# Two slots of a scan made in one tile, the product with B issued for both at once, and the projection weights loaded pass by pass

## The chip, the cores and the metric

The kernel runs on one core of a Trainium2 chip. The metric is device time in microseconds (us), from the first to the last instruction of one launch. A core has five engines that run their own instruction streams in order: PE (TensorE, matrix products), DVE (VectorE), ACT (ScalarE), POOL (GpSimd) and SP (SyncE, which here issues every DMA). They meet through semaphores. SBUF is the on-chip memory of 128 partitions, PSUM holds the results of PE in banks.

## What is computed

Two layers on an image of 8 samples, 512 channels and 48 x 48 = 2304 positions. Layer 0 adds to x a linear attention with a causal sum over the positions (8 heads of 64 channels). Layer 1 adds a chain of four state-space blocks, one for each 128 channels. Each layer first normalizes x by groups of 16 channels.

```python
# layer 0, with x0 = _gn(x)
q  = einsum('nchw,oc->nohw', x0, Wq) + bq ;  kv = einsum('nchw,oc->nohw', x0, Wkv) + bkv
Q, K = elu(q) + 1, elu(k) + 1                    # per head, positions in order
num = q_l . sum_{m<=l} k_m v_m^T ;  den = 1 / (Q . cumsum(K) + 1e-10)
x = x + num * den
# layer 1, block i of 4, on x_i = spx[i] + prev
xz = u @ Wi.T ;  xp, z = split(xz)               # 256 inner channels d
xs = silu(causal_conv4(xp) + bc)
dt, Bm, Cm = split(xs @ Wx.T)                    # 8, 16 and 16 rows
delta = softplus(dt @ Wdt.T + bdt)
h_l = exp(delta_l * A) * h_(l-1) + (delta_l * xs_l) * Bm_l      # 256 x 16 states
y = (h . Cm + xs * D) * silu(z) ;  x_m = y @ Wo.T
fused = max(x_i, x_m) ; feature = sigmoid(mean(x_i)) * x_i + sigmoid(mean(fused)) * fused
```

The state of layer 1 is a recurrence over 2304 positions for each of 8 samples x 4 blocks x 256 channels x 16 states. It is most of the work around the change.

## The kernel before

**Jobs and slots.** A sample's 2304 positions are cut into `NC` = 6 chunks of `LC` = 384. A *job* is one chunk of one block of one sample: 8 x 4 x 6 = 192 jobs. Two streams (even and odd samples) take turns; a stream's jobs follow one another, since each needs the last states of the one before. A job has `SLOTS` = 8 slots, 1536 in all. A slot holds four scans of 128 partitions x 384 positions: `NG` = 2 pairs of states, times 2 groups of channels. Slots 0 to 3 belong to one half of the channels, 4 to 7 to the other, and slot s uses state group s % 4.

**One slot.** The tile `u` holds the input of the four scans, then their result, then the result times C:

- `last_product` (L849): ACT copies the states kept from the chunk before into column 0 (L855), POOL makes the product of B and `dxr` for the last `TAIL` = 128 positions (L856);
- `product` (L864): DVE makes it for the first 256 positions (L867);
- `decay` (L873): ACT makes exp(delta A) into a PSUM bank (L877), `DEPTH` = 3 of them ahead;
- `scan` (L885): DVE runs the recurrence in place (L888), four times a slot;
- `weigh` (L898): POOL saves the last state (L902) and multiplies the tile by C in place (L904);
- `gather` (L908): PE adds it into `yp` (L911).

**Order.** The order on each engine is written out by hand in `slot` (L1130). In slot k it first issues `product` for slot k+1, then the four scans of slot k. After the second scan it issues the `gather` of slot k-2, then `last_product` for slot k+2 (L1161), and after the scans `weigh`. So POOL gets, slot after slot: product for k+2, other work, `weigh` of k. At slot 7 both of the next job's first two `product`s are issued (L1164). `u` has five buffers. `prime` (L1120) makes the first two slots where nothing was issued ahead.

**Work beside the slots.** Other work is written as generators that yield the place where they go on; a place is a half slot. `beside` (L1051) is called twice a slot and lets those go on that are due and find PSUM banks. `hurry` forces them. `Job.prepare` (L681) makes conv, gate, xs and delta of a job and loads its inputs. With `first` = twice the job's first slot, its DMAs go out at fixed half slots: steps of delta `dr` (`steps`), delta times xs `dxr` (`scaled`) and the rows of B and C, each spread over 64 partitions from a scratch tensor in DRAM (`rows`, L794). There are four tiles of B and four of C for a job, one for each state group, of two rows each; tile q serves slots q and q + 4. A tile takes two DMAs of 192 KB. Before that, delta goes to DRAM (`spread`, L771), POOL multiplies it by xs in place (L805) and it goes to DRAM again. Stores wait in a list and are issued by `flush` (L167) two half slots later. All DMAs are on the queue of SP.

**Attention.** `chunk` (L273) does one of 192 chunks (sample b, 128 output channels o, chunk c) of layer 0: three projections on PE (L293) with weights from `wq_sb`, and the rest of the attention in some thirty half slots. `statistics` (L216) makes the group sums of a sample; for the first sample it loads x whole into tiles of the tag `u`. The projection weights are all loaded at the start, 12 DMAs of 256 KB by `load_projections` (L106), into one tile of 4 x 1536 columns. `fetch` (L258) loads the normalized x of the next chunk.

The tiles are handed out by a pool: a tag has a number of buffers, and a new tile waits for the last user of the buffer that it takes. The waits between engines come from which parts of a tile an instruction reads and writes.

Of the kernel before, what the change touches and what calls it, by code (L numbers as in the profile page):

```python
# [9 lines left out]
F32 = mybir.dt.float32  # L10
# [7 lines left out]
P = 128  # L18
# [32 lines left out]
def attention_then_mamba_kernel(  # L51
# [50 lines left out]
    wq_sb = cpool.tile([P, 4, 1536], F32, name="wq_sb")  # L102
# [3 lines left out]
    def load_projections(o):  # L106

        src = wqkv.rearrange("(t p) c -> p t c", p=P)
        for j in range(3):
            cols = slice(j * 512 + o * P, j * 512 + (o + 1) * P)  # L110
            nc.sync.dma_start(out=wq_sb[:, :, cols], in_=src[:, :, cols])
# [104 lines left out]
    def statistics(b):  # L216
# [3 lines left out]
        if b == 0:  # L220

            xs = []

            def load(c):
                t = mpool.tile([P, 4, 1 + LC], F32, tag="u", name=f"xs_{c}", bufs=5)[:, :, 0:LC]
                nc.sync.dma_start(out=t, in_=xv[:, :, c * LC : (c + 1) * LC])
                xs.append(t)

            for c in range(5):
                load(c)  # L230
            load_projections(0)
            for c in range(NC):
                for ct in range(4):
                    nc.vector.bn_stats(stats[:, ct, c, :], xs[c][:, ct, :])
                if c == 0:
                    load(5)
                    fetch(0)
            for o in range(1, 4):
                load_projections(o)
# [33 lines left out]
    def chunk(m):  # L273
# [16 lines left out]
        def project(j):  # L290
            ps = bank()[:, 0:LC]
            for kt in range(4):
                nc.tensor.matmul(  # L293
                    ps,
                    wq_sb[:, kt, j * 512 + o * P : j * 512 + (o + 1) * P],
# [44 lines left out]
        fetch(m + 1)  # L340
        if o:
# [156 lines left out]
    class Stream:  # L498
# [62 lines left out]
        def pass_on(self):  # L561
# [52 lines left out]
            if last and self.z:  # L614

                got = [
                    mpool.tile([P, 4, 1 + LC], F32, tag="u", name=f"end_{i}", bufs=5)
                    for i in range(NC // 2)
                ]
                for c in range(NC):  # L620
# [53 lines left out]
    class Job:  # L674
# [6 lines left out]
        def prepare(self):  # L681
# [98 lines left out]
            src = scr.rearrange("(q i m f) l -> q m i (f l)", q=4, m=2, i=2)  # L780
# [13 lines left out]
            def rows(m, q):  # L794
                t = mpool.tile([P, NG, LC], F32, tag="BC"[m], name=f"{'BC'[m]}_{n}_{q}", bufs=4)
# [20 lines left out]
            rows(0, 1)  # L816
            self.prepared = True
            yield first - 3, 0
            rows(0, 2)
            yield first - 2, 0  # L820
            rows(1, 0)
            yield first - 1, 0
            rows(0, 3)
            yield first, 0
            rows(1, 1)
# [3 lines left out]
            rows(1, 2)  # L829
            yield first + 3, 0  # L830
            steps(1)
            yield first + 4, 0
            rows(1, 3)

        prepared = closed = False

# [12 lines left out]
        def last_product(self, s):  # L849

            shape, cols = [P, NG, 2, TAIL], slice(LC - TAIL, LC)
            u = mpool.tile([P, NG, 2, 1 + LC], F32, tag="u", name=f"u_{self.n}_{s}", bufs=5)
            if self.c:
                h, q = s // 4, s % 4 * NG
                nc.scalar.copy(u[:, :, :, 0], self.state[:, h, q : q + NG, :])  # L855
# [403 lines left out]
```

## Time and profile before

Three runs took 8785.19, 8786.02 and 8791.31 us, with a median of 8786.02. The profiled execution has a span of 8790.1 us.

| | us |
|---|---|
| median of three runs | 8786.02 |
| span of the profiled execution | 8790.1 |
| first scan | some 229 after the start |
| scans on DVE, L888, 6144 of 939 ns | 5457.0 |
| product with C on POOL, L904, 1536 of 3179 ns | 4882.7 |
| decays on ACT, L877, 6144 of 578 ns | 3413.6 |
| gather on PE, L911, 12288 of 519 ns | 2440.7 |
| product with B on POOL, L856, 1536 of 1277 ns | 1960.9 |
| product with B on DVE, L867, 1536 of 1195 ns | 1836.0 |
| projections on PE, L293, 4608 of 508 ns | 1680.1 |

How to read a group's line: line of the kernel, engine, operation, output and inputs by the program's names with their shapes, count, then busy time in all and the mean of one in ns, then the engine's idle time ahead of these instructions, and what ended it. A line of the waits reads: engine and line, what it waited for, us in total, how often, the longest. The chain is followed back from the last instruction to what released each step; its shares are shares of the span.

The 16 DMA engines are busy 69.0% of the span with the data queue and move 1642.98 MB, of which the rows of B and C are 3072 transfers of 192 KB.

### The profile page before, as it was taken

What the parts mean: (1) busy time and instruction counts of PE and PEld (TensorE: products, weight loads), DVE (VectorE), ACT (ScalarE), POOL (GpSimd) and SP (SyncE); (2) the same over time, 40 slices, a digit from 0 to 9 for tenths busy, and PEclk for the clock granted to TensorE, in tenths of its full rate; (3) what the DMA queues carried; (4) which work ended last, traced back from release to release, by engine and by line L of the source; (5) the groups of instructions that cost most, each with busy time, mean ns of one, the idle gap of its engine ahead of it and who ended that gap; (6) DMA issues with size and microseconds to landing.
All of it is one profiled execution on the core that took longest, in us unless ns stands there. A gap on an engine that the chain in (4) does not pass through costs nothing.

```text
span 8790.1 us, 122627 instructions
## 1 busy us (share of the span) xinstructions
PE 7766.8 (88%) x36482; PEld 3705.4 (42%) x36482; DVE 8067.0 (92%) x11078; ACT 6744.5 (77%) x13220; POOL 8044.8 (92%) x5623
## 2 busy tenths in 40 slices
PE   7899999998899899998889999999888999999865
PEld 4444444444444444444444444444444444444422
DVE  2899999999899999998889999999889999999998
ACT  2777887777788878777778878877777888877875
POOL 1789999999999999999999999999999999999998
PEclk9999999999999999999999999999999999999977
DMA  5667777766676777776667677777667666766655
GB/s 184 166 174 189 193 197 195 190 188 186 190 191 188 191 195 198 196 190 189 179 190 192 188 191 198 198 195 188 188 183 191 189 187 187 189 187 185 183 156 144
DMA packets 1002907, 1642.98 MB, mean 187 GB/s; under 512 B 138592, under 2 KB 797312, under 8 KB 1002240
## 3 DMA queue, kind: packets, MB, share of 16 engines
q1 hardware_dynamic: 1002240, 1635.13, 69.0%
q8 instruction: 291, 4.77, 0.2%
q14 instruction: 376, 3.08, 0.1%
HBM read 1309.06 MB, written 325.58 MB: 186 GB/s over the span
## 4 chain that ended last, share of the span: by engine, by line
DVE 28%; POOL 20%; ACT 14%; DMA 13%; PE 13%; issue 7%; SPq 4%; POOLq 0%; DVEq 0%; ACTq 0%
DVE u L888 19%; POOL u L904 11%; ACT bank L877 5%; DVE u L867 5%; POOL u L856 4%; PE bank L693 4%; PE bank L293 3%; PE yp L911 3%; DMA C<-scr 3%; SPq L797 2%; DMA dscr<-delta 2%; ACT L877 2%; DMA B<-scr 1%; ACT L764 1%; POOL delta L805 1%
## 5 line engine op out<-in xcount | busy, mean ns | idle before, releaser
L888 DVE TENSOR_TENSOR_SCAN u<-bank,u 128x385 f32<-128x385 f32 (+1 forms) x6144 | 5457.0, 939 | 350.1 <-ACT bank L877 300.3
L904 POOL TENSOR_TENSOR u<-u,C 128x1536 f32<-128x1536 f32 x1536 | 4882.7, 3179 | 121.9 <-DVE gm_m L182 16.9
L877 ACT ACTIVATE bank<-dr,av 128x385 f32<-128x385 f32 (+1 forms) x6144 | 3413.6, 578 | 752.3 <-DVE u L888 611.9
L911 PE MATMUL yp<-u,cst 128*64 128x384 f32 x12288 | 2440.7, 519 | 428.2 <-POOL u L904 355.9
L856 POOL TENSOR_TENSOR u<-B,dxr 128x512 f32<-128x512 f32 x1536 | 1960.9, 1277 | 16.5 <-DMA dxr<-xscr 13.8
L867 DVE TENSOR_TENSOR u<-B,dxp 128x1024 f32<-128x1024 f32 x1536 | 1836.0, 1195 | 11.3 <-ACT dxp L840 11.1
L293 PE MATMUL bank<-xn,wq_sb 128*128 128x384 f32 x4608 | 1680.1, 508 | 82.2 <-POOL xn L317 40.1
L911 PEld LDWEIGHTS yp<-u,cst 128*64 128x64 f32 x12288 | 782.0, 140 | 1660.6 <-issue 842.6
L693 PE MATMUL bank<-xi,wk 128*128 128x384 f32 x3072 | 1117.8, 507 | 218.5 <-ACT kl L390 112.5
L293 PEld LDWEIGHTS bank<-xn,wq_sb 128*128 128x128 f32 x4608 | 849.0, 195 | 826.5 <-DVE u L888 119.6
L693 PEld LDWEIGHTS bank<-xi,wk 128*128 128x128 f32 x3072 | 560.6, 192 | 780.8 <-ACT kl L390 202.1
L805 POOL TENSOR_TENSOR delta<-delta,xs 128x384 f32<-128x384 f32 x384 | 384.4, 1001 | 278.0 <-DMA dscr<-delta 215.9
L305 ACT ACTIVATE ex<-bank,bqkv_sb 128x384 f32<-128x384 f32 x384 | 221.0, 576 | 523.8 <-PE bank L293 523.6
L877 ACT ACT_TABLE_LOAD x382 | 490.1, 1283 | 6.7
L845 ACT ACTIVATE yp<-xs,pv 128x384 f32<-128x384 f32 x384 | 223.8, 583 | 290.8 <-DVE yz L923 289.3
L902 POOL COPY state<-u 128x4 f32<-128x4 f32 x1280 | 242.4, 189 | 172.6 <-DVE u L888 170.0
L753 PE MATMUL bank<-dbc,wd 9*128 9x384 f32 x768 | 315.6, 532 | 1.2 <-ACT dbc L745 1.1
L929 PE MATMUL bank<-yz,wo 128*128 128x384 f32 x768 | 299.2, 506 | 18.5 <-DVE yz L923 14.6
L704 PE MATMUL bank<-xi,wi 128*128 128x384 f32 x768 | 285.9, 494 | 10.9 <-ACT xs L729 10.9
L740 PE MATMUL bank<-xs,wx 128*40 128x384 f32 x768 | 281.0, 489 | 2.6 <-ACT sm L457 2.6
L923 DVE TENSOR_TENSOR yz<-yp,sz 128x384 f32<-128x384 f32 x384 | 211.6, 551 | 62.5 <-PE yp L911 62.3
L423 PE MATMUL bank<-cst,rdb 128*128 128x128 f32 x576 | 113.0, 311 | 170.7 <-DVE u L888 168.5
(117 smaller groups left out, 8018.7 us busy)
## 6 DMA issues: line engine op xcount, KB each, us to landing
B<-scr SPq DMA_DIRECT2D x1536, 192.0 KB
C<-scr SPq DMA_DIRECT2D x1536, 192.0 KB
xn<-xn SPq DMA_DIRECT2D x192, 768.0 KB
dr<-dscr SPq DMA_DIRECT2D x768, 192.0 KB
dxr<-xscr SPq DMA_DIRECT2D x768, 192.0 KB
dscr<-delta SPq DMA_DIRECT2D x192, 384.0 KB
xscr<-delta SPq DMA_DIRECT2D x192, 384.0 KB
xn<-in_x SPq DMA_DIRECT2D x48, 768.0 KB
```

The costliest lines, as they stand in the source:

```text
L293: nc.tensor.matmul(ps, wq_sb[:, kt, j * 512 + o * P : j * 512 + (o + 1) * P], xn[:, kt, :], start=(kt == 0), stop=(kt == 3),)
L693: nc.tensor.matmul(xc, wk[:, k, h * P : (h + 1) * P], xi[:, c0 + k : c0 + k + LC], start=(k == 0), stop=(k == 3),)
L704: nc.tensor.matmul(zp, wi[:, 256 + h * P : 256 + (h + 1) * P], xi[:, c0 + 3 : c0 + 3 + LC], start=True, stop=True,)
L753: nc.tensor.matmul(vp, wd[32:41, h * P : (h + 1) * P], dbc[32:41, :], start=True, stop=True)
L805: nc.gpsimd.tensor_tensor(delta[:, h, :], delta[:, h, :], xs[:, h, :], ALU.mult)
L856: nc.gpsimd.tensor_tensor(u[:, :, :, 1 + LC - TAIL :], self.B[s % 4][:, :, cols].unsqueeze(2).to_broadcast(shape), self.dxr[s // 4][:, :, ...
L867: nc.vector.tensor_mul(u[:, :, :, 1 : 1 + LC - TAIL], self.B[s % 4][:, :, cols].unsqueeze(2).to_broadcast(shape), self.dxp.unsqueeze(1).to ...
L877: nc.scalar.activation(dA[:, cols], self.dr[h][:, g, cols], AF.Exp, scale=self.w[6][:, 2 * h + g, q + j : q + j + 1],)
L888: nc.vector.tensor_tensor_scan(u[:, j, g, cols], dA[:, cols], u[:, j, g, cols], 0.0, ALU.mult, ALU.add,)
L904: nc.gpsimd.tensor_tensor(h, h, self.C[s % 4].unsqueeze(2).to_broadcast([P, NG, 2, LC]), ALU.mult)
L911: nc.tensor.matmul(self.yp[g * 64 : g * 64 + 64, 0:LC], pair_sum, u[:, j, g, 1:], start=False, stop=(s % 4 == 3 and j == NG - 1), skip_gro ...
L929: nc.tensor.matmul(self.xm[:, 0:LC], self.w[2][:, h, :], self.yz[:, h, :], start=(h == 0), stop=(h == 1),)
```

## The change

`u` tiles hold two slots (8 scans) instead of one, and there are three buffers of them instead of five. `last_product` is called at even slots alone and issues one ACT copy and one POOL product for both slots; `product`, the scans, `weigh` and `gather` stay one a slot. The tiles of B and C hold four rows, two buffers each instead of four; tile q now serves slots 2q, 2q + 1, 2q + 4 and 2q + 5. Their loads go from 16 a job to 8 of twice the size, at fewer places. The projection weights come as one contiguous load for each of the 32 passes over a sample's 128 output channels, in a tile with two buffers, asked for at the last chunk but one of the pass before; the host lays them out for that. At the start the six tiles of x are all loaded before the weights.

```diff
-    wq_sb = cpool.tile([P, 4, 1536], F32, name="wq_sb")
-    def load_projections(o):
-        src = wqkv.rearrange("(t p) c -> p t c", p=P)
-        for j in range(3):
-            cols = slice(j * 512 + o * P, j * 512 + (o + 1) * P)
-            nc.sync.dma_start(out=wq_sb[:, :, cols], in_=src[:, :, cols])
+    wqs = []
+    def load_projections():
+        i = len(wqs)
+        if i < 4 * B:
+            o = parts[i * NC][1]
+            w = apool.tile([P, 4, 3 * P], F32, tag="wq", name=f"wq_{i}", bufs=2)
+            nc.sync.dma_start(out=w.rearrange("p t c -> p (t c)"), in_=wqkv[o])
+            wqs.append(w)
...
             def load(c):
-                t = mpool.tile([P, 4, 1 + LC], F32, tag="u", name=f"xs_{c}", bufs=5)[:, :, 0:LC]
+                if c % 2 == 0:
+                    both = mpool.tile([P, 8, 1 + LC], F32, tag="u", name=f"xs_{c}", bufs=3)
+                    halves.append(both)
+                t = halves[c // 2][:, c % 2 * 4 : c % 2 * 4 + 4, 0:LC]
...
-            for c in range(5):
+            for c in range(NC):
                 load(c)
-            load_projections(0)
+            load_projections()
...
-                    load(5)
                     fetch(0)
-            for o in range(1, 4):
-                load_projections(o)
...
-                    wq_sb[:, kt, j * 512 + o * P : j * 512 + (o + 1) * P],
+                    wqs[m // NC][:, kt, j * P : (j + 1) * P],
...
         fetch(m + 1)
+        if c == NC - 2:
+            load_projections()
...
-            src = scr.rearrange("(q i m f) l -> q m i (f l)", q=4, m=2, i=2)
+            src = scr.rearrange("(q i m f) l -> q m i (f l)", q=2, m=2, i=2)
...
             def rows(m, q):
-                t = mpool.tile([P, NG, LC], F32, tag="BC"[m], name=f"{'BC'[m]}_{n}_{q}", bufs=4)
+                t = mpool.tile([P, 2 * NG, LC], F32, tag="BC"[m], name=f"{'BC'[m]}_{n}_{q}", bufs=2)
...
             yield first - 5, 0
-            rows(0, 1)
             self.prepared = True
             yield first - 3, 0
-            rows(0, 2)
+            rows(0, 1)
             yield first - 2, 0
             rows(1, 0)
-            yield first - 1, 0
-            rows(0, 3)
-            yield first, 0
-            rows(1, 1)
             yield first + 1, 0
             scaled(1)
             yield first + 2, 0
-            rows(1, 2)
+            rows(1, 1)
             yield first + 3, 0
             steps(1)
-            yield first + 4, 0
-            rows(1, 3)
+        def part(self, tiles, s):
+            return tiles[s % 4 // 2][:, s % 2 * NG : s % 2 * NG + NG]
...
         def last_product(self, s):
-            shape, cols = [P, NG, 2, TAIL], slice(LC - TAIL, LC)
-            u = mpool.tile([P, NG, 2, 1 + LC], F32, tag="u", name=f"u_{self.n}_{s}", bufs=5)
+            shape, cols = [P, 2 * NG, 2, TAIL], slice(LC - TAIL, LC)
+            u = mpool.tile([P, 2 * NG, 2, 1 + LC], F32, tag="u", name=f"u_{self.n}_{s}", bufs=3)
             if self.c:
                 h, q = s // 4, s % 4 * NG
-                nc.scalar.copy(u[:, :, :, 0], self.state[:, h, q : q + NG, :])
+                nc.scalar.copy(u[:, :, :, 0], self.state[:, h, q : q + 2 * NG, :])
             nc.gpsimd.tensor_tensor(
                 u[:, :, :, 1 + LC - TAIL :],
-                self.B[s % 4][:, :, cols].unsqueeze(2).to_broadcast(shape),
+                self.B[s % 4 // 2][:, :, cols].unsqueeze(2).to_broadcast(shape),
                 self.dxr[s // 4][:, :, cols].unsqueeze(1).to_broadcast(shape),
                 ALU.mult,
             )
-            return u
+            return [u[:, 0:NG], u[:, NG : 2 * NG]]
...
-        for r in range(2):
-            us[k + r] = job.last_product(s + r)
+        us[k], us[k + 1] = job.last_product(s)
...
                 if not end and k + 2 < slots and not apart(k + 2):
                     j, r = at(k + 2)
-                    us[k + 2] = j.last_product(r)
+                    if s % 2 == 0:
+                        us[k + 2], us[k + 3] = j.last_product(r)
```

`product` and `weigh` read their part of B and C through `part`. The rows of the projection that gives B and C, and the projection weights, are laid out on the host to match. The last block's end, which borrows tiles of the tag `u`, takes parts of two of the larger tiles.

More of the change, by code (lines that the diff above doesn't have):

```diff
@@ L220, in statistics @@
         if b == 0:
-            xs = []
+            xs, halves = [], []
             def load(c):
-                t = mpool.tile([P, 4, 1 + LC], F32, tag="u", name=f"xs_{c}", bufs=5)[:, :, 0:LC]
+                if c % 2 == 0:
+                    both = mpool.tile([P, 8, 1 + LC], F32, tag="u", name=f"xs_{c}", bufs=3)
+                    halves.append(both)
+                t = halves[c // 2][:, c % 2 * 4 : c % 2 * 4 + 4, 0:LC]
                 nc.sync.dma_start(out=t, in_=xv[:, :, c * LC : (c + 1) * LC])
                 xs.append(t)
-            for c in range(5):
+            for c in range(NC):
                 load(c)
-            load_projections(0)
+            load_projections()
             for c in range(NC):
@@ L616, in pass_on @@
                 got = [
-                    mpool.tile([P, 4, 1 + LC], F32, tag="u", name=f"end_{i}", bufs=5)
-                    for i in range(NC // 2)
+                    mpool.tile([P, 2 * NG, 2, 1 + LC], F32, tag="u", name=f"end_{i}", bufs=3).rearrange(
+                        "p a b l -> p (a b) l"
+                    )
+                    for i in range(2)
                 ]
+                got = [got[0][:, 0:4], got[0][:, 4:8], got[1][:, 0:4]]
                 for c in range(NC):
@@ L868, in product @@
                 u[:, :, :, 1 : 1 + LC - TAIL],
-                self.B[s % 4][:, :, cols].unsqueeze(2).to_broadcast(shape),
+                self.part(self.B, s)[:, :, cols].unsqueeze(2).to_broadcast(shape),
                 self.dxp.unsqueeze(1).to_broadcast(shape),
@@ L904, in weigh @@
             nc.gpsimd.tensor_tensor(
-                h, h, self.C[s % 4].unsqueeze(2).to_broadcast([P, NG, 2, LC]), ALU.mult
+                h, h, self.part(self.C, s).unsqueeze(2).to_broadcast([P, NG, 2, LC]), ALU.mult
             )
@@ L1225 @@
         8 + 16 * m + 2 * (q + j) + i
-        for q in range(0, 8, NG)
+        for q in range(0, 8, 2 * NG)
         for i in range(2)
         for m in range(2)
-        for j in range(NG)
+        for j in range(2 * NG)
     ]
@@ L1233 @@
         "consts": constants(),
-        "wqkv": lay(np.concatenate([wq, wkv], axis=0).T),
+        "wqkv": lay(
+            np.concatenate([wq, wkv], axis=0)
+            .reshape(3, 4, P, 4, P)
+            .transpose(1, 4, 3, 0, 2)
+            .reshape(4, P, 4 * 3 * P)
+        ),
         "bqkv": lay(np.concatenate([bq, bkv]).reshape(12, P).T),
```

## The prediction

> **What bounds the kernel now.** I read the page's busy line first, then the groups, the chain, the windows and the waits. Two engines stand level, and a third is close:
>
> ```profile
> PE 7766.8 (88%) x36482; PEld 3705.4 (42%) x36482; DVE 8067.0 (92%) x11078; ACT 6744.5 (77%) x13220; POOL 8044.8 (92%) x5623
> DVE 28%; POOL 20%; ACT 14%; DMA 13%; PE 13%; issue 7%; SPq 4%; POOLq 0%; DVEq 0%; ACTq 0%
> DVE u L888 19%; POOL u L904 11%; ACT bank L877 5%; DVE u L867 5%; POOL u L856 4%; PE bank L693 4%; PE bank L293 3%; PE yp L911 3%; DMA C<-scr 3%; SPq L797 2%; DMA dscr<-delta 2%; ACT L877 2%; DMA B<-scr 1%; ACT L764 1%; POOL delta L805 1%
> ```
>
> DVE and POOL are both busy 92% of 8790.1 us. The chain that ended last moves among all engines, with no more than 28% on one of them. So a saving on POOL alone does not come through whole.
>
> The windows say where each is the tighter one (columns: window, length, busy of PE, weight load, DVE, ACT, POOL, clock, DMA share, GB/s):
>
> ```profile
> 1826.70:2387.20 560.50, 490.47 (x2267) 229.93 (x2267) 503.33 (x693) 421.62 (x830) 523.05 (x384) 0.95 0.69 188
> 2914.60:3440.70 526.10, 477.24 (x2286) 229.66 (x2285) 504.88 (x694) 423.35 (x831) 497.69 (x342) 0.99 0.73 194
> 8259.40:8790.00 530.60, 349.83 (x1272) 134.26 (x1271) 471.35 (x579) 357.96 (x693) 496.74 (x334) 0.81 0.57 155
> ```
>
> Each of the first two holds 96 slots. The first has more POOL work and takes 34.4 us longer with the same DVE work: POOL leads there (93.3% against 89.8%), as in the last window. Two more windows are like the first (from 3968.5 and 6117.5 us). In the other twelve or so, DVE is at about 96% and POOL at 95%. So about 384 slots are POOL's, and 1152 are DVE's first.
>
> What DVE waits for, over the whole run:
>
> ```profile
> DVE u L888 <- ACT bank L877: 300.3, 212, 4.4
> DVE q L350 <- ACT bank L306: 102.4, 57, 6.0
> DVE yz L923 <- PE yp L911: 62.3, 39, 6.6
> DVE u L888 <- POOL u L856: 49.0, 41, 2.9
> ```
>
> It waits directly for POOL only 49.0 us. But late POOL products also hold PE (the waits list gives 951 us of PE and its weight loads on L904), PE holds ACT, and ACT's decays hold the scans. Part of the first three lines is POOL's.
>
> **The change, part by part.** The prices:
>
> ```profile
> L904 POOL TENSOR_TENSOR u<-u,C 128x1536 f32<-128x1536 f32 x1536 | 4882.7, 3179 | 121.9 <-DVE gm_m L182 16.9 <-DVE u L888 0.9 <-DMA B<-scr 0.4
> L856 POOL TENSOR_TENSOR u<-B,dxr 128x512 f32<-128x512 f32 x1536 | 1960.9, 1277 | 16.5 <-DMA dxr<-xscr 13.8 <-DMA B<-scr 2.7
> L805 POOL TENSOR_TENSOR delta<-delta,xs 128x384 f32<-128x384 f32 x384 | 384.4, 1001 | 278.0 <-DMA dscr<-delta 215.9 <-ACT bank L877 33.3 <-ACT sm L457 18.8
> L539 POOL TENSOR_TENSOR wk<-wk,wi 128x256 f32<-128x256 f32 x128 | 93.2, 730 | 7.1 <-DMA wk<-in_wconv 3.6 <-DMA av<-in_alog 3.4
> L855 ACT COPY u<-state 128x4 f32<-128x4 f32 x1280 | 238.6, 186 | 5.7 <-PE yp L911 3.0
> ```
>
> (1) **POOL, the product with B.** 1536 instructions of 512 elements become 768 of 1024. No row has 1024. From 256 to 384 to 512 elements an element costs (1001-730)/128 = 2.12 and (1277-1001)/128 = 2.16 ns; from 512 to 1536 it costs (3179-1277)/1024 = 1.86 ns. So one pair costs between 1277+512x1.86 = 2228 and 1277+512x2.16 = 2381 ns, against 2x1277 = 2554. The saving is 173 to 326 ns a pair, 133 to 250 us in all. No row lies nearer, so I take the middle: 2305 ns, 249 ns a pair, 191 us, or 0.125 us a slot. A loss is excluded by the same rows: at no size does the next element cost more than the mean one (2.49 ns at 512).
>
> The Trainium skill's "GPSIMD Engine Reference" (section 3.1) speaks against this: it counts two-input work on this engine as some 2.6 cycles per element, 4497 ns for 2048 elements, so that merging would save only what is not per element. By it 512 elements are 1109 ns, 168 of the measured 1277 are fixed, and the saving would be an estimated 129 us, which would put the forecast some 25 us later. L904's 2.07 ns per element, below the page's 2.17, says that longer instructions run cheaper than that.
>
> How much reaches the end: in POOL's 384 slots 48 us are saved, and I let 70% through (POOL still waits there for the delta store, L805: 26.4 of 560.5 us in the first window): 34 us. In the other 1152 slots 144 us are saved; there DVE has only 4% idle, some 21 us a window or 255 us over 12, less than half of it traceable to POOL, so 30%: 43 us. Sum 77.
>
> (2) **The order on POOL.** The product for an odd slot is now made one slot earlier, that for an even one ends 1.03 us later (2305-1277). I paired the records of L856 and L888 slot by slot: the scan began within 40 ns of the product's end (DVE stood waiting) in 23 jobs at slot 5, 30 at slot 7, and in none at even slots; less than 1.03 us was left at even slots in 20 jobs of 192. So most of the 49.0 us go; as part of it is the same time as in (1), 18 us. Each even L904 starts about 1 us later, each odd one a quarter us earlier. What is queued behind on PE is the gather (L911): it began within 0.1 us of the end of L904 in 83% of the jobs at slot 7 (odd, helped) and 2, 24, 12 and 26% at slots 0, 2, 4, 6. Priced at nothing; the cover is PE's 12% of idle.
>
> (3) **ACT.** 1280 copies of 186 ns become 640 of eight elements. If the price stays fixed 119 us are saved, if it doubles nothing. ACT has 23% idle: 6 us.
>
> (4) **Row loads.** 3072 DMAs of 192 KB become 1536 of 384 KB; SP issues 1536 x 0.587 us less, on a queue that is not the bound: nothing gained. The waits move, though. A tile now serves slots 0, 1, 4, 5 or 2, 3, 6, 7. The first C load must wait for L904 of slot 5 and the second for that of slot 7. Counted from the next job's first scan, SP issues the first at -7.1 us (median) and that L904 ends at -5.8; the second -- at its place +2.1, the L904 at +3.6, 95% by +7.2. SP thus stands 1 to 5 us there; behind it stand the second half's dxr and dr loads and then the delta store, which is issued at +8.7. Cover: the first C rows are read at +5.0, the second at +16.9, and a pair of loads lands 3.8 us after its issue now (90%: 5.6), 1.4 to 2.4 us more when doubled. Without it SP would delay the delta store, and POOL behind it at L805. Nothing.
> What is not covered so well: the doubled B load goes ahead of the first half's dxr load. A 384 KB pair of rows takes 2.4 us; at the 270 GB/s of busy stretches it is 1.4 us, so dxr lands 1.4 to 2.4 us later. From its issue to ACT's copy of it (L840) there are 5.1 us at the 5th percentile, 7.1 at the 25th, 8.5 at the median. At a landing of 5.2 to 8 us some 15 to 20% of the 192 jobs wait about 1 us, 30 to 40 us, half of it shared with waits there anyway: minus 15. Bounds: 0, and 192 x 1.4 = 269.
>
> (5) **Projection weights.** 12 DMAs of 256 KB at the start become one of 768 KB for each of the 32 passes: 25.2 MB for 3.1. That is 22 MB more on 1643, 1.3%, on engines with a 69% share; each is asked for one to two chunks (5 to 16 slots) before its use and reuses a buffer left five chunks ago. Cost 0 to 31 x 2.8 us if each one displaced other loads; I take 4.
>
> (6) **Start.** The sixth x tile was issued at 12.5 us, behind three weight loads, and DVE waited 2.84 us for it; nine further weight loads held SP for 10.46 us. 0 to 5 us, I take 3.
>
> Sum: 77+18+6-15-4+3 = 85. 8790.1-85 = 8705 for a profiled run; the median of the runs is 4.1 us below the span, so **8701**.
>
> **The rivals.**
> *Almost all of POOL's saving comes through* (a POOL-paced kernel whose other waits are echoes): 191 + 18 + half of (3), less 19: 8540 to 8600. For it: 951 us of PE waiting for POOL. Against: DVE at 96% in most windows.
> *It is hidden*: the chain has 4% on L856, 352 us; a pair is 9.8% cheaper, 34 us, and the costs of (4) and (5) at 19 to 40 take that: 8770 to 8800. For it: the chain's spread over engines; against: the last window, where POOL is at 94% and DVE 89%.
> *Slower: dxr behind the doubled B rows.* ACT stands at L840 in its own order, with the decays of the next slots behind it, and DVE's first product of the job behind those. The forecast without this term gains 100; from 0.52 us a job (100/192) on, it loses. At 1 us: 8786-100+192 = 8878. For it: loads go out in bursts, with the DMA share at nine tenths and more, and this one is the tightest of the job; against: L867 waited for L840 only 11.1 us in all, and three quarters of the jobs have 7 us.
> *The halves of a u tile are treated as one*, so that a scan waits for the product and gather of its neighbour: over 3 us a slot, above 12000. Against: paired slot by slot, three quarters of L867 begin before the L856 that writes other columns of the same tile has ended, so parts are told apart.
>
> **The numbers.** Forecast 0.55 (own range 8640 to 8765), comes through 0.10, hidden 0.12, slower 0.21, halves 0.02. About 0.2% (18 us) can be told from no change. Faster: 0.55+0.10+0.03 of hidden; same 0.09; slower 0.23 with the two last and the edge. The range goes to 8600, a part of the second case, and to 8830, a part of the slower one: some 0.8.
>
> **What would show it.** Right: L856 x768 at 2.2 to 2.4 us; POOL busy 130 to 250 us less; DVE's wait for L856 below 20 us; the windows with POOL ahead shrinking most. Wrong: L840 idle on dxr of 100 us and more; SP held on C rows with L805's wait well above 278 us; L856 at 2.5 us; DVE's idle unchanged though POOL's busy time fell.

## The result, and the profile after

The changed kernel takes 8823.12 us (median of 7 runs, 8818.76 to 8829.54), the kernel before 8799.74 us (median of 7 runs, 8785.19 to 8808.23). The medians are 23 us apart; the ratio, which is taken from all the runs, is 1.0033, with a 95% interval of 1.0022 to 1.0043: about 29 us slower, a small loss and a sure one. The time lies inside the range forecast; the sign of the forecast was wrong. The median of the kernel before differs by some 14 us between groups of runs, so what follows compares ratios; 0.001 is 8.8 us.

The busy line and the groups of the changed kernel (group: line, engine, operation, output and inputs, count, then busy time and mean, then idle time before and its main releaser):

```profile
span 8819.8 us, 117507 instructions
PE 7782.8 (88%) x36482; PEld 3711.8 (42%) x36482; DVE 8065.6 (91%) x11078; ACT 6703.8 (76%) x12580; POOL 7941.6 (90%) x4855
...
L908 POOL TENSOR_TENSOR u<-u,C 128x1536 f32<-128x1536 f32 x1536 | 4883.8, 3180 | 138.5 <-DVE gm_m L184 28.8
...
L860 POOL TENSOR_TENSOR u<-B,dxr 128x1024 f32<-128x1024 f32 x768 | 1818.7, 2368 | 21.7 <-DMA dxr<-xscr 18.6
```

The instruction did what it says: 768 products of 1024 elements in place of 1536 of 512. POOL is busy 103 us less (8044.8 before), ACT 41 us less, DVE the same to 2 us. Yet the span is 29.7 us longer. An engine works less and the kernel ends later, so something else now stands in a worse place. The waits of the changed kernel (engine, line, what it waited for, us in all, times, longest):

```profile
DVE u L892 <- ACT bank L881: 364.1, 224, 5.6
DVE yz L927 <- PE yp L915: 78.0, 36, 7.6
DVE u L871 <- ACT dxp L844: 23.8, 19, 7.8
POOL state L906 <- DVE u L892: 283.8, 153, 10.7
PE bank L701 <- POOL xi L675: 147.6, 83, 4.8
ACT dxp L844 <- DMA dxr<-xscr: 38.2, 32, 9.9
ACT kl L395 <- PE bank L391: 59.8, 27, 5.6
POOL delta L813 <- DMA dscr<-delta: 132.2, 52, 25.6
```

The row of `kl` in the kernel before:

```profile
ACT kl L390 <- PE bank L386: 22.1, 21, 5.1
```

DVE waits 64 us more for ACT's decays (300.3 before) and 16 us more for the gather (62.3). It waits no longer for the product with B: that row of 49.0 us is down to 0.8. POOL's saved time has become waiting for DVE: 283.8 us against 170.0. Two rows name a chain that the forecast had not followed. PE's convolution waits 147.6 us for `xi`, the input of the next block, which POOL makes with two adds, against 103.2 before. And ACT waits 59.8 us, against 22.1, for `kl`, a copy for the attention, whose source PE makes in matmuls (L391) that stand right behind that convolution in the timeline of the changed kernel below.

I measured each slot from its first scan to that of the next slot, as a mean over the 192 jobs. Slots 0 to 4 and 6 are shorter by 4 to 170 ns each, 315 ns together; slot 5 is 66 ns longer and slot 7 443 ns (6731 to 7174 ns). The balance is 194 ns a job, 37 us over all jobs: the loss lies in slot 7. POOL's idle time, counted the same way, shows where its saving went: in slots 4 to 6 it is under 0.1 us a slot in both kernels, but it grows from 0.93 to 1.28 us in slot 3 and from 0.61 to 1.15 us in slot 7. In slot 7 the fourth scan starts as its decay ends in 97% of the jobs, in both kernels: ACT sets that slot. ACT works in the order of its program, and ahead of that decay it has `kl` and the Silu work of a later job there, which both come behind PE's convolutions.

So the convolutions are looked at next. Timelines of PE show one place, the first convolution of a new channel tile, that is of the next block's 128 channels (start, duration, operation; in brackets the idle time before and who ended it). The eight matmuls of a line are records of the trace: four products in the code, two records each. Before, and the changed kernel:

```profile
3031.97 1.51 PE L911 MATMUL yp<-u,cst 128*64 128x384 f32 x8
3035.87 4.41 PE L693 MATMUL bank<-xi,wk 128*128 128x384 f32 x8 [2.38 <-POOL xi L667]
...
3042.44 2.85 PE L693 MATMUL bank<-xi,wk 128*128 128x384 f32 x8
```

```profile
3026.29 1.51 PE L915 MATMUL yp<-u,cst 128*64 128x384 f32 x8
3031.30 4.54 PE L701 MATMUL bank<-xi,wk 128*128 128x384 f32 x8 [3.50 <-POOL xi L675]
3035.68 0.49 PE L391 MATMUL bank<-cst,k 128*128 128x128 f32 x3
...
3037.87 2.85 PE L701 MATMUL bank<-xi,wk 128*128 128x384 f32 x8
```

The same eight matmuls take 2.85 us at one time and 4.4 to 4.5 us at another, each time after an idle stretch. The windows of the changed kernel around it (after the window and its length: busy of PE, weight load, DVE, ACT, POOL, then the granted clock, DMA share, GB/s) say why:

```profile
3024.00:3030.00 6.00, 3.81 (x24) 1.55 (x20) 6.00 (x7) 4.62 (x11) 5.92 (x4) 1.00 0.88 207
3030.00:3036.00 6.00, 4.70 (x11) 2.65 (x12) 6.00 (x9) 2.47 (x5) 5.92 (x6) 0.72 0.46 128
3032.00:3035.00 3.00, 3.00 (x6) 1.65 (x5) 3.00 (x5) 1.89 (x4) 2.92 (x3) 0.50 0.57 172
3036.00:3042.00 6.00, 6.00 (x27) 3.00 (x26) 4.45 (x6) 4.79 (x8) 5.22 (x3) 1.00 1.00 222
```

The granted clock averages 0.72 over the 6 us with the long convolution; inside it, over 3 us, it is 0.50, and it is back at 1.00 in the next window. In the trace's clock records this drop is to half speed for 3.41 us, and it begins 0.66 us after the convolution does. I counted the 384 convolutions of each kernel by the idle time in front of them and call one of over 3.5 us *long*:

| idle before the convolution | before: all, long | after: all, long |
|---|---|---|
| 1.0 to 2.0 us | 78, 2 | 75, 5 |
| 2.0 to 3.0 us | 20, 8 | 1, 1 |
| 3.0 to 3.4 us | 1, 1 | 2, 1 |
| 3.4 to 4.0 us | 1, 1 | 21, 20 |
| over 4.0 us | 1, 1 | 2, 2 |
| all 384 | 14 long | 29 long |

Those with under 1.0 us are left out of the rows (283 in each kernel, 1 of them long before). The long ones with under 2.0 us, but for one after, lie in the last 430 us, where the clock was already low before the idle stretch; without that end the counts are 10 and 22. The share of the row from 2.0 to 3.0 us is itself unsteady: among some 20 such stretches, 2 are long in e3, 3 in e5, 6 in e11 and 11 in e12 (runs below).

The timeline of POOL in the changed kernel shows what delays `xi`:

```profile
3023.56 2.39 POOL L860 TENSOR_TENSOR u<-B,dxr 128x1024 f32<-128x1024 f32 x1
3025.89 1.01 POOL L670 TENSOR_TENSOR fu<-fu,xi 128x384 f32<-128x384 f32 x1
3026.83 0.21 POOL L906 COPY state<-u 128x4 f32<-128x4 f32 x1
3027.11 3.18 POOL L908 TENSOR_TENSOR u<-u,C 128x1536 f32<-128x1536 f32 x1
3030.24 1.01 POOL L675 TENSOR_TENSOR xi<-xb,fu 128x384 f32<-128x384 f32 x1
```

The product made in slot 4 (2.39 us in place of 1.28) stands ahead of the first add (`fu`), of slot 4's product with C and so of `xi`. PE has ended the gather of an earlier slot at 3027.8 and makes no other matmul until `xi` is there. Its idle stretch grows from 2.4 to 3.5 us, and with it the clock goes from "sometimes falls" to "nearly always falls". The Trainium skill's "TensorE: Matmul & The Clock Gate" (part 1, the clock gate) says that the array goes to the throttled clock after an idle window of about 3.4 us, and that the window runs free of the kernel. The 20 of 21 at 3.4 to 4.0 us agree; the 8 of 20 at 2.0 to 3.0 us do not fit a rule that needs a whole idle window, and there the measurement decides. That the drop *costs* the time is so far an argument; the last two runs test it.

### The profile page after: what moved, and what is told of

Same layout as the page of the kernel before. It is cut to its first block, busy times and chain, and to the rows that moved or that the text cites. A ratio compares the mean times of both kernels' runs of the same rounds, so it can differ in the third digit from the quotient of the medians.

```text
span 8819.8 us, 117507 instructions
## 1 busy us (share of the span) xinstructions
PE 7782.8 (88%) x36482; PEld 3711.8 (42%) x36482; DVE 8065.6 (91%) x11078; ACT 6703.8 (76%) x12580; POOL 7941.6 (90%) x4855
## 5 line engine op out<-in xcount | busy, mean ns | idle before, releaser
L860 POOL TENSOR_TENSOR u<-B,dxr 128x1024 f32<-128x1024 f32 x768 | 1818.7, 2368 | 21.7 <-DMA dxr<-xscr 18.6
L296 PE MATMUL bank<-xn,wq 128*128 128x384 f32 x4608 | 1679.1, 507 | 108.1 <-POOL xn L320 63.5
L701 PE MATMUL bank<-xi,wk 128*128 128x384 f32 x3072 | 1149.0, 519 | 252.5 <-POOL xi L675 147.6
L296 PEld LDWEIGHTS bank<-xn,wq 128*128 128x128 f32 x4608 | 843.1, 193 | 855.8 <-DVE u L892 113.6
L813 POOL TENSOR_TENSOR delta<-delta,xs 128x384 f32<-128x384 f32 x384 | 385.7, 1005 | 282.2 <-DMA dscr<-delta 132.2
L906 POOL COPY state<-u 128x4 f32<-128x4 f32 x1280 | 244.7, 191 | 289.1 <-DVE u L892 283.8
```

The source lines that it names most:

```text
L296: nc.tensor.matmul(ps, wqs[m // NC][:, kt, j * P : (j + 1) * P], xn[:, kt, :], start=(kt == 0), stop=(kt == 3),)
L701: nc.tensor.matmul(xc, wk[:, k, h * P : (h + 1) * P], xi[:, c0 + k : c0 + k + LC], start=(k == 0), stop=(k == 3),)
L813: nc.gpsimd.tensor_tensor(delta[:, h, :], delta[:, h, :], xs[:, h, :], ALU.mult)
L860: nc.gpsimd.tensor_tensor(u[:, :, :, 1 + LC - TAIL :], self.B[s % 4 // 2][:, :, cols].unsqueeze(2).to_broadcast(shape), self.dxr[s // 4][: ...
```

## The experiments

Each ratio is against the kernel before in the same group of runs, with its 95% interval.

| run | what it is | us | ratio |
|---|---|---|---|
| e1 | changed kernel, all small work ahead of the pair's product | 9129.59 | 1.0391 [1.0377, 1.0405] |
| e2 | changed kernel, dxr loads ahead of B | 8832.66 | 1.0047 [1.0034, 1.0060] |
| e3 | changed kernel, two products at the old places | 8849.17 | 1.0069 [1.0056, 1.0081] |
| e4 | changed kernel, C rows loaded as before | 8825.07 | 1.0036 [1.0024, 1.0048] |
| e5 | kernel before, weights pass by pass | 8798.75 | 1.0002 [0.9993, 1.0011] |
| e6 | changed kernel, B in halves at the old places | 8856.67 | 1.0068 [1.0054, 1.0082] |
| e7 | changed kernel, two products, both at even slots | 8862.36 | 1.0075 [1.0062, 1.0087] |
| e8 | changed kernel, all B and C loads as before | 8807.37 | 1.0019 [1.0010, 1.0028] |
| e9 | e8, slot 4's small work ahead of the product | 8796.89 | 1.0009 [1.0001, 1.0018] |
| e10 | changed kernel, the same move | 8815.72 | 1.0032 [1.0020, 1.0045] |
| e11 | e8, two products at the old places | 8794.02 | 1.0001 [0.9992, 1.0010] |
| e12 | kernel before, the same move | 8794.83 | 1.0002 [0.9994, 1.0011] |
| e13 | e9, no half slot between the two adds for xi | 9122.59 | 1.0378 [1.0362, 1.0394] |
| e14 | kernel before, the same joining | 9472.29 | 1.0765 [1.0750, 1.0780] |
| e15 | e10, the same joining | 9483.96 | 1.0787 [1.0772, 1.0802] |
| e16 | kernel before, shorter product with C | 8737.73 | 0.9937 [0.9925, 0.9950] |
| e17 | e9, PE kept at work ahead of the convolution | 8776.27 | 0.9983 [0.9974, 0.9992] |
| e18 | changed kernel, the same | 8794.23 | 1.0006 [0.9997, 1.0015] |

### The parts of the change one by one (e3, e4, e5, e8, e11)

**e5: the weights alone**, on the kernel before.

```diff
-            load_projections(0)
+            load_projections()
...
-            for o in range(1, 4):
-                load_projections(o)
...
-                    wq_sb[:, kt, j * 512 + o * P : j * 512 + (o + 1) * P],
+                    wqs[m // NC][:, kt, j * P : (j + 1) * P],
...
+        if c == NC - 2:
+            load_projections()
```

> The kernel before with the projection weights loaded pass by pass (and the start's order) and nothing else of the change. Theory W (the weights' loads cost the loss): 8810-8850. Theory D (B rows of two slots and dxr come late together): within 8 us of before, or a few us below it by the shorter start.

1.0002 [0.9993, 1.0011]: the weights are worth nothing either way.

**e3: the changed kernel with one product a slot** at the places of before; tiles and loads stay doubled.

```diff
-            return [u[:, 0:NG], u[:, NG : 2 * NG]]
+            return u
...
-                    if s % 2 == 0:
-                        us[k + 2], us[k + 3] = j.last_product(r)
+                    us[k + 2] = j.last_product(r)
```

> The changed kernel, its tiles and loads kept, with two products of 512 elements at the places of before (one each slot) in place of one of 1024. Theory P: POOL gets its 142 us back, and yet the time goes back to that of before, 8790-8805, or below. Theory D and S: the loads are the cause, the saving is lost on top: 8830-8870.

1.0069. Taking the merged product away makes the changed kernel slower, so with the doubled loads the merging is a gain of some 32 us. The waits of e3:

```profile
ACT dxp L844 <- DMA dxr<-xscr: 46.3, 41, 8.4
DVE u L875 <- ACT dxp L844: 33.2, 26, 7.2
```

ACT's copy waits 46.3 us for dxr (8.1 before), DVE's first product behind it 33.2 us (11.1). The doubled B load does make dxr late, as the forecast said.

**e4: the C rows as before**, four tiles and eight loads a job, with only B doubled.

```diff
-            rows(1, 0)
+            c_rows(0)
+            yield first, 0
+            c_rows(1)
...
-            rows(1, 1)
+            c_rows(2)
...
+            yield first + 4, 0
+            c_rows(3)
```

> The changed kernel with the C tiles and their loads as before (four tiles of two rows, 192 KB loads at four places). Theory S: SP's 697 us of waiting for the product with C go, and the time falls to 8790-8805. Theories P and D: SP's waiting goes, the time stays within 8 us of 8823.

1.0036, the same as the changed kernel's 1.0033. SP's queue does stand behind POOL for the C tiles in the changed kernel, but nothing that matters is behind it. Its waits there:

```profile
SPq L805 <- POOL u L908: 697.5, 369, 7.1
```

**e8: B and C loads as before, merged product kept**, and **e11: the same with one product a slot**. Both keep the tiles of two slots; e8 loads a B tile in halves.

```diff
-            rows(0, 0)
+            b_rows(0, 0)
...
+            b_rows(0, 1)
             self.prepared = True
...
-            rows(0, 1)
+            b_rows(1, 0)
...
+            b_rows(1, 1)
```

> The changed kernel with all loads of B and C as before (192 KB, eight places, four tiles of C), B put into tiles of two slots. The merged product, the u tiles and the weights of the change stay. Theories D and S together: 8755-8785, faster than before. Theory W: 8810-8830.

> e8_loads_as_before with two products of 512 elements at their old places: of the change only the u and B tiles of two slots and the weights are left. If the tiles cost nothing, within 8 us of before (8797); the 56 us by which e3_two_products lay above before are then the loads' alone. If the tiles themselves cost: 8805-8850.

e11 is 1.0001: tiles of two slots and three buffers cost nothing. e8 is 1.0019 [1.0010, 1.0028]: the merged product by itself, with all loads as before, makes the kernel slower by some 16 us against e11 (the two intervals just touch), though POOL is busy 101 us less (8042.3 to 7941.1). The doubled loads cost 0.0068 with two products (e3 against e11), but 0.0014 with the merged one (changed kernel against e8; the intervals overlap). So the loss can be told in two orders: loads first, some 60 us lost and 32 won back by merging; merging first, some 16 us lost and 12 more by the loads. The parts don't add up singly; that one hides the other's cost is all that I can say of it.

### Where the product stands, and the order of the loads (e1, e2, e6, e7)

**e7: two products again, but both at the even slot**, everything else as in the changed kernel.

```diff
-            nc.gpsimd.tensor_tensor(
-                u[:, :, :, 1 + LC - TAIL :],
...
+            for r in range(2):
+                nc.gpsimd.tensor_tensor(
+                    u[:, r * NG : r * NG + NG, :, 1 + LC - TAIL :],
```

> The changed kernel with two products of 512 elements issued together at even slots, in place of one of 1024. If the gain over e3_two_products comes from the order (the odd product a slot earlier), the time stays within 10 us of 8823; if it comes from the 186 ns a pair that POOL saves, it goes to 8840-8860.

1.0075. At one place and with the same loads, merging gives 0.0042, some 37 us, for 106.5 us of POOL's busy time (8048.1 to 7941.6): 35%. So the saving on POOL does come through in part. Moving both to the even slot costs little against e3 (1.0075 and 1.0069, the intervals overlap), though its long convolutions are 29 against e3's 11. This speaks against a fixed price for a long convolution: in this pair 18 more of them come with some 5 us, and whether something else that the move gains hides their cost was not told apart.

**e2: dxr loads first**, ahead of the steps and of B.

```diff
+            scaled(0)
             steps(0)
-            rows(0, 0)
             yield first - 6, 0
-            scaled(0)
+            rows(0, 0)
```

> The changed kernel with the load of the first half's dxr issued ahead of the steps and the B rows. Theory D: ACT's wait for dxr (38.2 us) goes, DVE's wait for ACT's copy (23.8 us) goes, and 20 to 50 us of time: 8775-8803. Theories P and S: the waits go, but the time by less than 15 us: 8808-8825.

1.0047, not better than the changed kernel. The wait only changed its name; the waits of e2:

```profile
DVE u L871 <- DMA B<-scr: 66.6, 48, 6.9
...
ACT dxp L844 <- DMA dxr<-xscr: 4.5, 1, 4.5
```

dxr is on time (4.5 us, once), and now the doubled B rows are late.

**e6: B in halves, C doubled.**

```diff
-            rows(0, 0)
+            b_rows(0, 0)
...
+            b_rows(0, 1)
...
             rows(1, 0)
+            yield first - 1, 0
+            b_rows(1, 1)
```

> The changed kernel with the B tile of two slots loaded in two halves at the four places of before: half, dxr, half. Theory D: DVE's waits for ACT's copy of dxr and for B go below 15 us in all, ACT's wait for dxr too, and the time falls by 15 to 40 us, 8783-8808. Theory W: no more than 10 us from 8823.

1.0068, worse, and with another cause. The waits of e6:

```profile
POOL u L875 <- DMA B<-scr: 76.4, 44, 17.0
```

The last half of B now stands on SP's queue behind the doubled C load, which waits for POOL, and POOL waits for that half. What is queued behind SP's wait decides its cost: nothing that shows in e4's comparison, 76.4 us of POOL's waiting here.

**e1: all small work ahead of the merged product** at even slots.

```diff
+                if s % 2 == 0:
+                    beside(2 * k + 1)
                 if not end and k + 2 < slots and not apart(k + 2):
...
-                beside(2 * k + 1)
+                if s % 2:
+                    beside(2 * k + 1)
```

> The changed kernel with one swap: at even slots the work beside the slots is issued ahead of the product for two slots, not behind it. Theory P (the long product holds up POOL's small work and with it the conv on PE, the Silu on ACT and the last decay of slot 7): the wait of DVE for decays falls from 364 us to 320 or less and the time to 8770-8800. Theory D (dxr late behind the doubled B rows) and theory S (SP held on the C rows): no change, 8815-8830.

1.0391. The waits of e1:

```profile
POOL delta L813 <- DMA dscr<-delta: 300.5, 85, 24.8
...
DVE u L892 <- POOL u L860: 81.7, 62, 3.3
```

This tells nothing on the order of `xi`: POOL's delta product, which waits for a DMA store, moved ahead too, and the merged product stood behind that wait.

### The small work of slot 4 alone (e9, e10, e12)

`xi` is made at slot 4. Only there the small work goes ahead of the product, in e8, in the changed kernel and in the kernel before:

```diff
+                if s == 4:
+                    beside(2 * k + 1)
                 if not end and k + 2 < slots and not apart(k + 2):
...
-                beside(2 * k + 1)
+                if s != 4:
+                    beside(2 * k + 1)
```

> e8_loads_as_before with the swap of e1 at slot 4 alone: there POOL makes the next block's xi (1.0 us) ahead of the product for two slots (2.37 us), and the delta product, which waits for a DMA, keeps its place. Theory P: what is left of the loss is the conv waiting for xi behind the long product; DVE's wait for decays falls from 376 to 300-330 us, PE's wait for xi by 60 us or more, the time from 8807 to 8750-8790, below before. Rival R (the wait in slot 7 has another source, such as the gather behind the late product with C): no change within 8 us, or slower.

> The changed kernel, its loads kept, with the same swap at slot 4 alone. Theory P: faster than 8823 by 15 to 40 us, 8783-8808. Rival R: 8815 or more.

> The kernel before with the swap at slot 4 alone: a control for the two runs above. With the short product xi comes 1.28 us earlier. If the place of xi matters by itself, as theory P says, a gain of 5 to 30 us, 8767-8792; rival R: no gain or a loss.

e9 is 1.0009 against e8's 1.0019, e10 is 1.0032 against 1.0033, e12 is 1.0002: at most a small gain. The count tells why: 31 long convolutions in e9, 27 in e10, 18 in e12 (29, 29, 14 without the move). The move does not shorten PE's idle stretch, which is over 3.2 us in 23 places of e9 and of e10. POOL's timeline in e9 has the reason:

```profile
3019.51 1.00 POOL L670 TENSOR_TENSOR fu<-fu,xi 128x384 f32<-128x384 f32 x1
3020.46 2.37 POOL L888 TENSOR_TENSOR u<-B,dxr 128x1024 f32<-128x1024 f32 x1
...
3023.04 3.17 POOL L936 TENSOR_TENSOR u<-u,C 128x1536 f32<-128x1536 f32 x1
3026.18 0.99 POOL L675 TENSOR_TENSOR xi<-xb,fu 128x384 f32<-128x384 f32 x1
```

Only the first add came ahead of the product. The second, which makes `xi`, goes out a half slot later, behind the product with C, and that stands where it stood. In e11, with two products, the same place reads:

```profile
3028.01 1.51 PE L947 MATMUL yp<-u,cst 128*64 128x384 f32 x8
3031.92 2.85 PE L701 MATMUL bank<-xi,wk 128*128 128x384 f32 x8 [2.40 <-POOL xi L675]
```

Idle for 2.40 us, and the clock stays.

### Joining the two adds (e13, e14, e15)

To have `xi` earlier, the half slot between POOL's two adds was left out, in e9, in the kernel before and in e10:

```diff
                     nc.gpsimd.tensor_tensor(fu, fu, xi[:, icols], ALU.add)
-                    yield "2" if c and self.fresh and not last else "1", 0
+                    if last or self.fresh:
+                        yield "2" if c and self.fresh and not last else "1", 0
```

> e9 with POOL's two steps to xi (fu, then xi) put one behind the other, ahead of the product with C of slot 4 that stood between them. Theory K (at a change of block PE stands idle 3.5 us for xi, its clock then drops, the conv takes 4.5 us for 2.85 and the Silu and the last decay of slot 7 come 2.8 us later): the slow convs at block changes fall from some 20 to under 8, slot 7 in those jobs by 2 us or more, and the time to 8740-8770, below before. Rival N (PE's wait is hidden): 8790-8800.

> The kernel before with the same two steps joined. Theory K: it has 14 slow convs, half of them at block changes; 5 to 25 us faster, 8770-8788. Rival N: within 5 us of before.

> e10 (the changed kernel with its own loads, xi first) with the two steps joined. Theory K: 8816 falls by 25 to 50 us to 8766-8791. Rival N: 8808-8823.

1.0378, 1.0765 and 1.0787. The waits of e14:

```profile
ACT dxp L841 <- DMA dxr<-xscr: 607.2, 120, 8.4
...
DVE u L868 <- ACT dxp L841: 522.6, 115, 7.9
```

The kernel before loses as much as the changed one, and through dxr, which has nothing to do with `xi`. The half slot that was left out also moved what follows in the same generator, its stores among them. That these stand ahead of dxr on SP's queue is my guess; it wasn't tried. For the question at hand the three runs are void.

### What a microsecond less on POOL is worth (e16)

The kernel before, with the product with C on 372 of 384 positions (the first 12 of each chunk are left out):

```diff
-            h = u[:, :, :, 1:]
+            h = u[:, :, :, 13:]
...
-                h, h, self.C[s % 4].unsqueeze(2).to_broadcast([P, NG, 2, LC]), ALU.mult
+                h,
+                h,
+                self.C[s % 4][:, :, 12:].unsqueeze(2).to_broadcast([P, NG, 2, LC - 12]),
+                ALU.mult,
```

> The kernel before with the product with C left out for the first 12 of 384 positions (it leaves out that part of y): POOL saves about 48 x 1.86 = 89 ns a slot, 137 us in all, the amount that the merged product saved, with nothing moved. The prediction let 40% of such a saving through: 8740 (-55). If POOL's time is not what bounds the kernel: within 12 us of before.

The group in e16:

```profile
L904 POOL TENSOR_TENSOR u<-u,C 128x1488 f32<-128x1488 f32 x1536 | 4745.2, 3089 | 126.1 <-DVE gm_m L182 13.7 <-DMA dxr<-xscr 7.3 <-DVE u L888 1.4
```

3089 ns for 3179; POOL's busy time falls by 130.4 us (8044.8 to 7914.4) and the time by 0.0063, some 55 us. So some 42% of a saving on POOL passes through when it is taken evenly from every slot and nothing moves (34 to 51% by the interval of the ratio).

### Does the clock cost the time? (e17, e18)

Three products of constants go ahead of the first convolution of a channel tile, 32 times in all. They wait for no data and the convolution overwrites them. No other work is moved.

```diff
                 xc = bank()[:, 0:LC]
+                if h == 0 and c == 0:
+                    for k in range(3):
+                        nc.tensor.matmul(xc, ident, cst[:, 0:LC], start=True, stop=True)
```

> The kernel of the run with the delta product... of slot 4 after the xi work and the B and C loads as before (8796.9 us, 1.0009 of the kernel before), with one addition: ahead of the first convolution of a channel tile (chunk 0 only) TensorE makes three more 128x128 by 128x384 products of constants into the same bank, which the convolution then overwrites; they wait for nothing. Clock theory: TensorE stands idle for 3.5 us there until GpSimd delivers xi, and then makes the 8 matmuls in 4.54 us instead of 2.85; the three products (3 x 0.71 us) cut the idle stretch to some 1.3 us, the share of convolutions over 3.5 us falls from about 30 to under 8, the fourth scan of slot 7 two slots later starts 2.8 us earlier in each of some 20 blocks, and the time falls by 30 to 60 us, to 8737 to 8767 us (0.994 to 0.997). Rival: the slow convolution is a sign of a late xi and costs nothing of its own, or is hidden behind ScalarE: convolutions may get shorter, the time stays at 8790 to 8800 (0.999 to 1.001). Third: the products hold TensorE up where xi is early: 8800 to 8830.

> The changed kernel (8823 us) with the same three products of constants ahead of the first convolution of a channel tile, and nothing else. Clock theory: slow first convolutions fall from 29 to under 8 and the time by 30 to 60 us, to 8763 to 8793 us (0.997 to 1.000 of the kernel before): the clock is then most of the loss of the change, and the doubled loads the rest. Rival (the clock costs nothing of its own, the loads and the longer product cost all): 8813 to 8833 (1.002 to 1.004).

PE's timeline in e18, at the place shown above:

```profile
3034.73 1.51 PE L918 MATMUL yp<-u,cst 128*64 128x384 f32 x8
3036.17 2.20 PE L702 MATMUL bank<-cst 128*128 128x384 f32 x6
3039.71 2.85 PE L704 MATMUL bank<-xi,wk 128*128 128x384 f32 x8 [1.34 <-POOL xi L675]
```

The added work fills 2.20 us, 1.34 us of idle are left, and the convolution takes 2.85 us at full speed. The granted clock around it, and ACT's wait for `kl`, 59.8 us in the changed kernel:

```profile
3039.50:3042.50 3.00, 2.79 (x9) 1.67 (x10) 3.00 (x5) 1.97 (x5) 2.92 (x4) 1.00 0.30 86
ACT kl L395 <- PE bank L391: 23.7, 29, 4.9
```

`xi` is no earlier (where PE waited for it, it is ready 9.7 us after the start of slot 4, 9.6 in the changed kernel, both medians): PE does *more* work and the kernel gets faster. The long convolutions fall from 29 to 9 in e18, 6 of them in the last 430 us, and from 31 to 4 in e17. Slot 7's four scans take 6.91 us in place of 7.10 (e18) and 6.86 in place of 7.06 (e17); those over 9 us fall from 23 to 4 and from 24 to 5. The times: e18 is 1.0006 [0.9997, 1.0015] against the changed kernel's 1.0033, e17 0.9983 [0.9974, 0.9992] against e9's 1.0009: 24 and 23 us, each with some 12 us either way by these intervals. Both gained less than the 30 to 60 us expected and stayed above the times given for them, but the rival had nothing. The lower clock is shown to cost time; with it gone, the changed kernel can't be told from the kernel before.

How much of the 24 us the change itself had lost is not settled. 14 of the convolutions were long before it, and the kernel before with the same three products was not run. If each of the 20 convolutions that e18 shortens is worth the same, the 15 that the change made long are 18 us; that is an estimate. For nearly all of the 24 us speaks that e18 goes back to the kernel before in the places that the chain names: 4, 23 and 4 slots 7 of over 9 us (before, changed, e18), and 22.1, 59.8 and 23.7 us of waiting for `kl`. e17, the merged product with the loads as before, slot 4's small work first and PE kept at work, beats both kernels by a little; without that missing run this isn't shown to be owed to the merged product.

## Why the prediction was wrong

**The step that failed** is in (2): "Each even L904 starts about 1 us later, each odd one a quarter us earlier. What is queued behind on PE is the gather (L911) ... Priced at nothing; the cover is PE's 12% of idle." The shift was foreseen in its direction, not in its size: against the end of its slot's scans, the product with C starts 0.63, 0.51, 0.64 and 0.57 us later at slots 0, 2, 4 and 6, and 0.4 to 0.5 us earlier at the odd ones. Two things were missed. POOL's small work is queued there too, `xi` above all, and PE's convolution stands behind that, not only the gather. And PE's idle time is no cover where a longer idle stretch makes the work after it slower. Worth 18 to 24 us by e18, on the side of a loss. That is the part of the failure whose cause is shown; it is not the whole of the gap between forecast and result (see what stays open).

That the time lies within the range is no merit of the mechanism: the forecast's own range ended at 8765, and it was drawn up to 8830 for a part of the slower rival.

**(1), the price.** 2368 ns, inside the bounds of 2228 to 2381, near the dear end; 2305 was taken. That makes 186 ns a pair and 142 us by spans, not 191. POOL's busy time falls by 103 us only. In the records an instruction's span begins some 45 ns before its predecessor's ends (68.6 us over 1536 products before, 34.7 us over 768 after), and a span less is also an overlap less. So the term for POOL was nearly twice too large. The Trainium skill's "GPSIMD Engine Reference" (section 3.1), from which the prediction worked out 129 us, was nearer to the 142 than the middle of the rows.

**(1), how much comes through.** 77 of 191 us, 40%, was the estimate; e16 shows some 42% for an even saving and e7 35% for this one. The rate was right within what these runs can tell. On the true 103 us it makes some 42 us. The split by windows has the right sign only where POOL led: the stretches of 96 slots that POOL led, from slots 288, 672 and 1056, are 3.5, 4.7 and 1.6 us shorter, far less than forecast, and all the others together, the last stretch among them (some 1 us longer, against the forecast), some 46 us longer, where a gain of 43 had been forecast.

**(2), the late products.** Right: DVE's wait for them went from 49.0 to 0.8 us.

**(3).** 640 copies of 198 ns, 126.8 us in place of 238.6: nearly the fixed price, as at the upper end.

**(4).** SP stood 697.5 us for C rows, 1.9 us each time, within the 1 to 5 us foreseen, and POOL's wait for the delta store fell (215.9 to 132.2), so that "Nothing" holds, as e4 confirms. dxr came late as forecast: ACT waited 30 us more for it and DVE 13 us more behind that. The term of 15 us stands beside 0.0014, some 12 us, by the changed kernel against e8. It is no constant, though: with two products the same loads cost 0.0068, some 60 us, four times the term. Counted in that order, it is this term that was too small, and merging wins 32 us of it back.

**(5) and (6).** The weights cost nothing (e5; 4 us forecast). The first scan begins 6.4 us earlier (229.4 to 222.9), against 3.

**The rivals.** "Slower: dxr behind the doubled B rows" gave the right side by a mechanism that is at most part of it: with loads as before (e8) the kernel is still slower. e2 doesn't clear the loads, since with dxr ahead the doubled B rows came late instead; and with two products the doubled loads alone lose some 60 us (e3 against e11). "Comes through" and "hidden" are out, and so is the rival of halves treated as one.

**What stays open.** With the sizes as measured, the sum would be some 42 + 18 + 6 - 12 + 6 = 60 us of gain; the change lost 29, so 89 us are to be explained, and the clock accounts for 18 to 24: some 65 to 71 us, the larger part, stay open. In e18 slot 7's scans still take 0.24 us more than before (46 us over 192 jobs), where the decay is last. Of ACT's waits that the change made longer, the one for `kl` goes back in e18, but two that stand ahead of slot 7's last decay do not: for dxr (8.1 us before, 38.2 in the changed kernel, 38.8 in e18; 4.7 in e17, whose loads are as before) and for the attention's output from PE, `xr` (52.0, 80.8 and 92.2; 68.2 in e17). They are candidates; no run takes one of them out alone. Why the doubled loads cost five times as much with two products as with one is open too.

## What to carry to other kernels

Merging two instructions moves work as well as it saves overhead: list everything that is queued behind the longer instruction on its engine, the small work too, and follow each item to its reader on other engines. An idle share of TensorE is no cover by itself: ask how long the single idle stretches become, because a longer one can be paid again in slower matmuls (here 20 of 21 times at 3.4 to 4.0 us). A saving on one engine of several that are level is worth only a share (here some 42% when it fell evenly); a saving that makes every other slot later can be worth less than nothing.

## What the runs showed of the hardware

- The granted clock of TensorE fell to half (0.50 over a window of 3 us) at single idle stretches of 3.4 to 4.0 us in 20 of 21 cases of the changed kernel, and at 2.0 to 3.0 us in 8 of 20 of the kernel before; in the two places shown, eight matmul records then took 4.4 and 4.5 us in place of 2.85. Three products of constants in the stretch, 2.20 us, kept the clock up at the place shown and left 9 of 29 long convolutions.
- GpSimd's two-input product took 1277 ns for 512 elements, 2368 for 1024, 3089 for 1488 and 3179 for 1536. Its spans in the records overlap those before them by some 45 ns, so that a mean of one overstates what an instruction less saves.
